# Four common PSUM banks, rewritten timetables, a bias moved and the layer norm's steps put in one order, in a two-layer vision kernel

## The chip, the cores and the metric

The kernel runs on one core of one Trainium2 chip. The metric is the device time of one execution in microseconds, the median of repeated runs. A core has TensorE (PE in the profile; its weight loads are PEld), VectorE (DVE), ScalarE (ACT), GpSimd (POOL) and SyncE (SP), which here issues nearly all DMA transfers in one queue. Each engine takes its instructions in program order and waits for others by semaphores. PSUM, where PE writes its products, has eight banks of 512 fp32 columns; SBUF is the larger on-chip memory.

## What is computed

The input is x of 8 images, 256 channels and 48 x 48 points (2304 tokens), all fp32. Two layers, each `x = x + layer(group_norm(x))`, with 32 groups of 8 channels:

- Layer 0 projects each token to features and to a position (256 each, with bias). Positions are normalised, the similarity of all pairs of tokens in an image is formed (2304 x 2304), each token takes its 16 most similar tokens, and the softmax of these 16 similarities weighs their features.
- Layer 1 is twice: a layer norm over channels, then a Mamba block without residual: in-projection to 512 + 512, a causal convolution over four tokens, SiLU, projections to a step size dt, B and C (16 states), the scan `h = exp(dt A) h + dt B x`, `y = C h` over the tokens, the skip `D x`, the gate `silu(z)`, and an out-projection to 256.

```
x = x + L0(gn(x))          # top-16 attention by similarity
x = x + L1(gn(x))          # twice: layer norm, Mamba block
```

## The kernel before

Layer 0 of the first image runs alone at the start. After that layer 1 of image b and layer 0 of image b + 1 run side by side, in an order written out by hand (`manual_schedule`): the program's order is each engine's order.

Layer 1 of an image is cut into 12 *units*: 6 chunks of 384 tokens (T) by 2 depths, in a skewed order. A unit has 16 *steps*, each 32 of the 512 inner channels with their 16 states laid over 128 partitions (4 states a row, Q), and a step has two *parts* of two states. So a unit has 32 parts, called places here, 96 units have 3072, and the main loop at the end of the kernel walks over them with m. At each place:

- `decay(m + 1)`: ACT writes exp(dt A) into one of two PSUM areas (L877).
- every second place `make_bx`: POOL multiplies B by dt x for the step after next (L853), and `pool_part` multiplies the states of the step before by C (L920).
- `run_scan(m)`: DVE runs the scan (L892). The letter of the part in the string SHARE says who multiplies by C: with G the scan is left in SBUF and POOL's L920 does it for one or both parts of the step; with V the scan is written to PSUM and DVE multiplies at once (L894). There are three strings, by what runs beside the unit: units 1 to 9 of an image except the last image have the top-k of the next image beside them (the first string); the units 0, 10 and 11 of these images have its projections (the second); the last image has nothing (the third).
- the other operations of a unit stand in timetables, lists of (place, operation): `between` goes ahead of the scan of a place and `behind` after it; `between_spare` and `behind_spare` take their part wherever no top-k stands beside. Places count from the unit's own first scan; -35 is a place in the unit before the previous one.
- `ahead.go(m)` moves layer 0 of the next image on by one step. A block of 128 tokens takes 16 places; the list `within` says at which of them each operation stands.

Operations that the change and the prediction touch:

- `load_rep` (L625) loads the dt or dt x rows of one step in four DMAs (tiles dtr, dtxr; three of each), `load_bc` (L633) B or C in four, `load_d` (L738) the skip weights, `times_x` makes dt x on POOL (L801) and stores it and dt (L804), `split` stores B and C (L776).
- `softplus` (L787 to L796) loads ACT's table, makes the four step sizes of a unit (L790) and puts the matmuls of the last two (L781) in between; `silu_z` (L815 to L819) does the like for the gate.
- the layer norm: `affine` (ACT, the group norm of the input, L670), `mean` (PE, L679), `center` (DVE, L685), `square` (ACT, L692), `variance` (PE, L698), `root` and `root_end`, `spread_root` (PE, L225), `scale` (DVE, L715), `normal` (ACT, L728). In the spare tables of before, square stands ahead of center and normal ahead of scale.
- `finish` (L540, L544): DVE adds the attended features, their bias and x in two operations of 128 columns, and takes the statistics of the sum; `leave` (L973) adds the last residual.
- PSUM: `mm` and `mm0` hand out banks of one ring; a new tile takes a bank that the program has given back. In the main loop da has four banks, the ring three, and `po`, which gathers the weighted features of a block over some six places, one of its own. While layer 0 runs alone, the ring has five and po two.

Of the kernel before, what the change touches and what calls it, by code (L numbers as in the profile page):

```python
# [8 lines left out]
F32 = mybir.dt.float32  # L9
BF16 = mybir.dt.bfloat16  # L10
AF = mybir.ActivationFunctionType
ALU = mybir.AluOpType
# [3 lines left out]
P = 128  # L16
# [9 lines left out]
def tile_conv_preact(  # L26
# [18 lines left out]
    nc = tc.nc  # L45
    B, C, N = x.shape
# [173 lines left out]

# [36 lines left out]

    def layer0(b, left, pool, ps0, alone):
        def mm0(w, name):
            return ps0.tile([P, 512], F32, tag="mm", name=name, bufs=5 if alone else 3)[:, :w]  # L260

        more = 2 if alone else 1
        depth = 2 if alone else 1
# [271 lines left out]
        def finish(t):  # L535
            row = blocks[t]
            xr = row["xr"]

            for cb in range(CB):
                nc.vector.scalar_tensor_tensor(  # L540
                    xr[:, cb, :], row["pr"][:, cb * P : (cb + 1) * P], b_feat[:, cb : cb + 1],
                    xr[:, cb, :], ALU.add, ALU.add,
                )
# [417 lines left out]
    def leave(unit, cb):  # L961

        b, c, rows = unit["b"], unit["c"], slice(cb * P, (cb + 1) * P)
        if unit["d"] + 1 < DEPTH:
            v1 = unit["left"].setdefault("v1", {})
            if c not in v1:
                v1[c] = hbm.tile([C, T], F32, tag="v1", name=f"v1_{b}_{c}", bufs=2 * BEHIND)
            vo = keep.tile([P, T], F32, tag="dtx", name=f"vo_{unit['u']}_{cb}")
            nc.scalar.copy(vo, unit["pw"][cb])
            nc.sync.dma_start(v1[c][rows, :], vo)  # L970
        else:
            res = unit["res"]
            nc.vector.tensor_add(res[:, cb, :], res[:, cb, :], unit["pw"][cb])  # L973
            nc.sync.dma_start(out[b, rows, c * T : (c + 1) * T], res[:, cb, :])


# [7 lines left out]
        (10, load_rep, "dtx", 9), (21, load_rep, "dtx", 14), (11, gate, 0), (-29, spread_root),  # L984
        (0, times_x, 3), (-19, load_in, 5), (33, load_out), (8, load_rep, "dtx", 8), (-22, load_in, 0),
        (21, load_rep, "dt", 13), (-20, tap, 0), (-10, step_size, 1), (9, copy_z, 2), (-18, in_proj, 2),
        (2, load_rep, "dtx", 5), (10, sum_states, 0), (13, load_rep, "dt", 9), (29, gate, 2), (9, silu_z),
        (7, load_rep, "dt", 6), (19, load_rep, "dt", 12), (-6, load_rep, "dtx", 1), (-14, load_in, 7),
        (-30, root), (9, load_rep, "dt", 7), (4, load_d, 1), (-24, load_in, 3), (17, load_rep, "dt", 11),
        (14, load_rep, "dtx", 11), (-13, x_proj), (-17, load_in, 6), (-3, load_d, 0), (4, load_rep, "dtx", 6),  # L990
        (-4, load_rep, "dtx", 2), (-42, load_v),
    ]
    behind = [
        (-12, split), (-3, load_rep, "dt", 1), (3, in_proj, 4), (-10, step_size, 0), (-3, load_rep, "dt", 0),
        (-8, load_rep, "dtx", 0), (-15, tap, 3), (-1, load_rep, "dt", 2), (-28, scale),
        (16, load_rep, "dtx", 12), (11, load_rep, "dt", 8), (8, in_proj, 6), (17, sum_states, 1),
        (-14, silu_x), (25, load_rep, "dt", 15), (-37, affine), (1, times_x, 2), (7, copy_z, 0),
        (10, load_rep, "dtx", 10), (-17, tap, 2), (-10, softplus), (-16, in_proj, 3), (3, load_rep, "dt", 4),
        (-29, load_in, 2), (6, in_proj, 7), (35, gate, 3), (-2, load_rep, "dtx", 3), (8, copy_z, 1),
        (40, leave, 1), (22, load_rep, "dtx", 15), (-8, load_in, 4), (29, load_d, 3), (-37, mean),  # L1000
        (-19, taps, 0), (-19, in_proj, 1), (-10, load_bc, 0), (33, sum_states, 3), (-30, root_end),
        (-9, times_x, 0), (-20, load_in, 1),
    ]
    between_spare = [
        (-34, center), (24, sum_states, 2), (-34, variance), (-21, in_proj, 0), (38, out_proj, 0),
        (-15, taps, 2), (-14, taps, 3), (-35, square), (39, leave, 0), (20, load_rep, "dt", 14),
        (5, load_rep, "dt", 5), (-4, load_bc, 1), (38, out_proj, 1), (17, load_d, 2), (-17, tap, 1),
        (18, load_rep, "dtx", 13), (-8, times_x, 1), (19, gate, 1), (-22, normal), (9, load_rep, "dtx", 8),
        (1, load_rep, "dt", 3), (0, load_rep, "dtx", 4), (14, load_rep, "dt", 10), (6, load_rep, "dtx", 7),
        (10, load_rep, "dtx", 9), (-18, taps, 0), (12, load_rep, "dtx", 10), (20, load_rep, "dtx", 14),  # L1010
        (11, gate, 0), (-1, times_x, 2), (-22, spread_root), (-19, load_in, 5), (33, load_out),
        (-22, load_in, 0), (21, load_rep, "dt", 13), (-20, tap, 0), (-10, step_size, 1), (9, copy_z, 2),
        (-18, in_proj, 2), (2, load_rep, "dtx", 5), (10, sum_states, 0), (13, load_rep, "dt", 9),
        (29, gate, 2), (9, silu_z), (7, load_rep, "dt", 6), (19, load_rep, "dt", 12), (-6, load_rep, "dtx", 1),
        (-14, load_in, 7), (37, gate, 3), (-31, root), (9, load_rep, "dt", 7), (5, load_d, 1),
        (-24, load_in, 3), (17, load_rep, "dt", 11), (14, load_rep, "dtx", 11), (-13, x_proj),
        (-17, load_in, 6), (-3, load_d, 0), (4, load_rep, "dtx", 6), (-4, load_rep, "dtx", 2), (-42, load_v),
    ]
    behind_spare = [
        (-12, split), (-3, load_rep, "dt", 1), (4, in_proj, 4), (-10, step_size, 0), (-5, load_rep, "dt", 0),  # L1020
        (-8, times_x, 3), (-8, load_rep, "dtx", 0), (-15, tap, 3), (-1, load_rep, "dt", 2), (-21, scale),
        (16, load_rep, "dtx", 12), (11, load_rep, "dt", 8), (8, in_proj, 6), (17, sum_states, 1),
        (-14, silu_x), (25, load_rep, "dt", 15), (-39, affine), (6, copy_z, 0), (-17, tap, 2), (-10, softplus),
        (-16, in_proj, 3), (7, in_proj, 5), (3, load_rep, "dt", 4), (-27, load_in, 2), (6, in_proj, 7),
        (-15, taps, 1), (-2, load_rep, "dtx", 3), (8, copy_z, 1), (40, leave, 1), (22, load_rep, "dtx", 15),
        (-16, load_in, 4), (29, load_d, 3), (-38, mean), (-21, in_proj, 1), (-12, load_bc, 0),
        (33, sum_states, 3), (-31, root_end), (-9, times_x, 0), (-25, load_in, 1),
    ]
    place = {(f, *args): part for part, f, *args in between + behind}

# [102 lines left out]
```

## Time and profile before

| | us |
|---|---|
| median of 3 runs | 9807.86 (9806.04 to 9808.63) |
| the profiled execution's own time | 9813.77 |
| its span | 9812.0 |
| first scan of the main loop starts at | 461.1 |
| DVE busy in the span | 8904.6 |
| POOL busy | 9023.9 |
| PE busy | 7958.7 |
| ACT busy | 7304.4 |

The profile is of one execution. Its page gives busy time by engine, the chain of work that ended last, and groups of equal instructions; a row of a group has the line, the engine, the operation, what it writes and reads, the shapes, the count, the busy time in us and the mean ns of one, and the idle time of the engine before it with what ended that. A row of the view of waits has engine and line that waited, what it waited for, the total in us, how often, and the longest. A row of the timeline has start and duration in us. Records of successive instructions of an engine overlap by some tens of ns, so the cost of one more instruction is read from the distance of starts.

### The profile page before, as it was taken

What the parts mean: (1) busy time and instruction counts of PE and PEld (TensorE: products, weight loads), DVE (VectorE), ACT (ScalarE), POOL (GpSimd) and SP (SyncE); (2) the same over time, 40 slices, a digit from 0 to 9 for tenths busy, and PEclk for the clock granted to TensorE, in tenths of its full rate; (3) what the DMA queues carried; (4) which work ended last, traced back from release to release, by engine and by line L of the source; (5) the groups of instructions that cost most, each with busy time, mean ns of one, the idle gap of its engine ahead of it and who ended that gap; (6) DMA issues with size and microseconds to landing.
All of it is one profiled execution on the core that took longest, in us unless ns stands there. A gap on an engine that the chain in (4) does not pass through costs nothing.

```text
span 9812.0 us, 133959 instructions
## 1 busy us (share of the span) xinstructions
PE 7958.7 (81%) x36761; PEld 4336.7 (44%) x36761; DVE 8904.6 (91%) x7864; ACT 7304.4 (74%) x15938; POOL 9023.9 (92%) x3971
## 2 busy tenths in 40 slices
PE   8888887888878887788877888778887788866665
PEld 6644443444434444444434445344443444422222
DVE  5599998999989999899988999899998999989898
ACT  4577877777777777777777787777786778767776
POOL 1199998999989999899999999999998999999999
PEclk9989998999989998899988999889998999977777
DMA  1244455545454445444454445544545454545554
GB/s 35 58 124 132 126 139 139 135 123 140 127 147 126 134 131 144 132 129 132 132 144 131 132 129 135 141 134 124 137 130 150 121 137 125 140 134 138 144 142 122
DMA packets 1241872, 1269.02 MB, mean 129 GB/s; under 512 B 266496, under 2 KB 1214208, under 8 KB 1241120
## 3 DMA queue, kind: packets, MB, share of 16 engines
q1 hardware_dynamic: 1240576, 1260.46, 47.7%
q8 instruction: 293, 4.80, 0.2%
q14 instruction: 459, 3.76, 0.1%
q10 hardware_dynamic: 544, 0.00, 0.0%
HBM read 1046.58 MB, written 212.86 MB: 128 GB/s over the span
## 4 chain that ended last, share of the span: by engine, by line
DVE 33%; ACT 24%; DMA 11%; PE 11%; SPq 10%; issue 7%; POOL 4%; ACTq 0%; DVEq 0%; POOLq 0%
DVE bx L892 11%; ACT da L877 10%; SPq L625 8%; DVE da L892 8%; DVE xc L751 5%; DMA dtr<-dt_d 4%; DVE bx L894 3%; DMA BC<-bc_d 3%; DVE top L464 2%; DVE left L467 2%; POOL bx L920 2%; PE po L514 2%; POOL bx L853 2%; DMA dtxr<-dtx_d 2%; ACT rest L486 1%
## 5 line engine op out<-in xcount | busy, mean ns | idle before, releaser
L853 POOL TENSOR_TENSOR bx<-BC,dtxr 128x1536 f32<-128x1536 f32 x1536 | 5296.3, 3454 | 144.5 <-PE y L938 72.8
L877 ACT ACTIVATE da<-dtr,A_sb 128x385 f32<-128x385 f32 x6144 | 3588.1, 584 | 868.6 <-DVE bx L892 375.1
L892 DVE TENSOR_TENSOR_SCAN bx<-da,bx 128x770 f32<-128x770 f32 x2073 | 3578.1, 1747 | 263.6 <-ACT da L877 232.4
L920 POOL TENSOR_TENSOR bx<-bx,BC 128x1536 f32<-128x1536 f32 (+1 forms) x1311 | 3353.6, 2558 | 70.5 <-DVE bx L892 66.0
L892 DVE TENSOR_TENSOR_SCAN da<-da,bx 128x770 f32<-128x770 f32 x999 | 1752.0, 1754 | 123.7 <-ACT da L877 81.2
L651 PE MATMUL pe<-vn,inw 128*128 128x384 f32 (+1 forms) x3072 | 1214.7, 526 | 329.6 <-issue 50.9
L514 PE MATMUL po<-feat,aT 128*128 128x256 f32 x5184 | 1352.3, 410 | 12.8 <-ACT aT L503 5.7
L938 PE MATMUL y<-bx,sel 128*32 128x384 f32 x12288 | 1266.0, 536 | 109.9 <-POOL bx L920 103.1
L443 PE MATMUL psim<-pos 128*128 128x512 f32 x2520 | 1215.2, 612 | 154.3 <-DVE xr L540 70.1
L514 PEld LDWEIGHTS po<-feat,aT 128*128 128x128 f32 x5184 | 1022.4, 203 | 343.1 <-issue 107.2
L894 DVE TENSOR_TENSOR bx<-da,BC 128x768 f32<-128x768 f32 x999 | 957.2, 958 | 34.4
L651 PEld LDWEIGHTS pe<-vn,inw 128*128 128x128 f32 x3072 | 566.9, 199 | 845.8 <-issue 206.2
L938 PEld LDWEIGHTS y<-bx,sel 128*32 128x32 f32 x12288 | 395.5, 118 | 961.5 <-issue 692.7
L443 PEld LDWEIGHTS psim<-pos 128*128 128x128 f32 x2520 | 478.0, 205 | 724.2 <-issue 375.5
L751 DVE SCALAR_TENSOR_TENSOR xc<-pe,cw,xc 128x384 f32<-128x384 f32 x1152 | 696.4, 611 | 43.4 <-ACT xc L743 16.3
L781 PE MATMUL pd<-dbl,dtp_sb 16*128 16x384 f32 x768 | 441.4, 689 | 336.5 <-ACT dt L790 189.9
L503 ACT ACTIVATE aT<-pt 128x512 f32<-128x512 f32 (+1 forms) x720 | 387.5, 548 | 419.8 <-PE pt L495 417.8
L956 PE MATMUL pw<-z,ow 128*128 128x384 f32 x1536 | 557.0, 509 | 112.8 <-ACT aT L503 52.4
L494 PE MATMUL pt<-ident,sim 128*128 128x128 f32 x2592 | 541.2, 290 | 18.5 <-ACT aT L503 13.6
L935 PE MATMUL y<-xc,dmat 128*128 128x384 f32 x768 | 398.3, 606 | 171.7 <-ACT h_st L930 58.5
L908 ACT COPY h_st<-da 128x2 f32<-128x2 f32 x808 | 128.6, 159 | 542.2 <-DVE bx L894 537.8
L495 PE MATMUL pt<-minus,rest 128*128 128x128 bf16 x2592 | 492.9, 224 | 5.9 <-ACT rest L486 5.8
(155 smaller groups left out, 9966.9 us busy)
## 6 DMA issues: line engine op xcount, KB each, us to landing
dtxr<-dtx_d SPq DMA_DIRECT2D x6144, 48.0 KB, 1.9
dtr<-dt_d SPq DMA_DIRECT2D x6144, 48.0 KB, 1.9
BC<-bc_d SPq DMA_DIRECT2D x768, 192.0 KB, 3.9
inw<-in_in_wT_dram SPq DMA_DIRECT2D x768, 128.0 KB, 2.3
dtx_d<-dtx SPq DMA_DIRECT2D x384, 192.0 KB, 2.3
dt_d<-dt SPq DMA_DIRECT2D x384, 192.0 KB, 2.3
ow<-in_out_wT_dram SPq DMA_DIRECT2D x96, 512.0 KB, 4.0
dmat<-diag SPq DMA_DIRECT2D x384, 64.0 KB, 2.2
```

Source lines behind the costliest of these rows:

```text
L443: nc.tensor.matmul(pm, pos[:, k, t * P : (t + 1) * P], pos[:, k, c0 : c0 + w], start=(k == 0), stop=(k == CB - 1),)
L514: nc.tensor.matmul(row["po"], aT[:, m % PT, :], feat[:, m, :], start=(m == 0), stop=(m == NB - 1))
L625: nc.sync.dma_start(rows[j * G : (j + 1) * G], src[:, i0, :])
L651: nc.tensor.matmul(pe, w[:, k], unit["vn"][:, k, lo:], start=(k == 0), stop=(k == CB - 1))
L751: nc.vector.scalar_tensor_tensor(unit["xc"][e], unit["pe"][e][:, k : k + T], cw[:, unit["d"], e, k : k + 1], unit["xc"][e], ALU.mult, ALU.add,
L853: nc.gpsimd.tensor_tensor(bx[:, :, 1:], unit["BC"][0], unit["dtxr"][i].unsqueeze(1).to_broadcast([P, Q, T]), ALU.mult,)
L877: nc.scalar.activation(da[:, s * (1 + T) : (s + 1) * (1 + T)], unit["dtr"][i], AF.Exp, scale=A_sb[:, unit["d"], i, p * HQ + s : p * HQ + s ...
L892: nc.vector.tensor_tensor_scan(h, da, g, 0.0, ALU.mult, ALU.add)
L894: nc.vector.tensor_tensor(bx[:, :, 0:T], da.rearrange("p (q t) -> p q t", q=HQ)[:, :, 1:], unit["BC"][1][:, qs], ALU.mult,)
L920: nc.gpsimd.tensor_tensor(g[:, :, 0:T], g[:, :, 1:], unit["BC"][1][:, qs], ALU.mult)
L938: nc.tensor.matmul(y[j * G : (j + 1) * G, :], sel, unit["bx"][k * J + j][:, q, 0:T], start=False, stop=True, skip_group_check=True,)
L956: nc.tensor.matmul(pw, unit["ow"][:, k, cb * P : (cb + 1) * P], unit["z"][k], start=(k == 0), stop=(k == DB - 1),)
```

## The change

- SHARE: in the first string place 29 goes from G to V, in the second 1 and 23 go from G to V, and 26 from V to G; in the third 11, 15 and 25 go from G to V, and 14, 18 and 27 from V to G.
- PSUM: the ring has four banks in the main loop and seven while layer 0 runs alone, and po takes its tile from it.
- The bias of the features is no longer added in `finish`; one sum of 256 columns takes the place of the two operations. The mean of the group norm gets it instead (`more` in `group_stats`), its shift is (bias - mean) x rstd, and `leave` adds it with the last residual.
- Timetables: `load_rep` of dt x 14 goes from place 21 to 19 (in the spare tables from 20 to 17), of dt 15 from 25 to 28, `affine` from -37 to -39, `times_x` of 2 from 1 to 2. In the spare tables center goes from -34 to -36, spread_root from -22 to -26 and scale from -21 to -25, so that center stands ahead of square, and scale ahead of normal.

```diff
     SHARE = (
-        "GGVGGGVVGGGGGGVGGGVVGGGVGGGGGGVG",
-        "GGGGVGVVGVVVGVGVGGGGVGVGGVVVGVGV",
-        "VGVGVGVGVGVGGGVGGGVVVGVVGGVVGGVG",
+        "GGVGGGVVGGGGGGVGGGVVGGGVGGGGGVVG",
+        "GVGGVGVVGVVVGVGVGGGGVGVVGVGVGVGV",
+        "VGVGVGVGVGVVGGGVGGGVVGVVGVVGGGVG",
     )
...
-    def group_stats(st, found, mm0, name):
+    def group_stats(st, found, mm0, name, more=None):
...
+        if more is not None:
+            nc.vector.tensor_add(mv[:, :, 0], mv[:, :, 0], more)
...
-        nc.gpsimd.tensor_mul(shift, mean, rstd)
-        nc.gpsimd.tensor_scalar(shift, shift, -1.0, None, ALU.mult)
+        if more is None:
+            nc.gpsimd.tensor_scalar(shift, mean, -1.0, None, ALU.mult)
+        else:
+            nc.gpsimd.tensor_sub(shift, more, mean)
+        nc.gpsimd.tensor_mul(shift, shift, rstd)
...
-            return ps0.tile([P, 512], F32, tag="mm", name=name, bufs=5 if alone else 3)[:, :w]
+            return ps0.tile([P, 512], F32, tag="mm", name=name, bufs=7 if alone else 4)[:, :w]
...
-                row["po"] = ps0.tile([P, 512], F32, tag="po", name=f"po_{b}_{t}", bufs=more)[:, :C]
+                row["po"] = mm0(C, f"po_{b}_{t}")
...
+            nc.vector.tensor_add(xr, xr, row["pr"].rearrange("p (k t) -> p k t", k=CB))
             for cb in range(CB):
-                nc.vector.scalar_tensor_tensor(
-                    xr[:, cb, :], row["pr"][:, cb * P : (cb + 1) * P], b_feat[:, cb : cb + 1],
-                    xr[:, cb, :], ALU.add, ALU.add,
-                )
                 nc.vector.bn_stats(st1[:, cb, t, :], xr[:, cb, :])
...
-        yield from group_stats(st1, found, mm0, f"b{b}")
+        yield from group_stats(st1, found, mm0, f"b{b}", b_feat)
...
-        return ps.tile([P, 512], F32, tag="mm", name=name, bufs=3)[:, :w]
+        return ps.tile([P, 512], F32, tag="mm", name=name, bufs=4)[:, :w]
...
-            nc.vector.tensor_add(res[:, cb, :], res[:, cb, :], unit["pw"][cb])
+            nc.vector.scalar_tensor_tensor(
+                res[:, cb, :], unit["pw"][cb], b_feat[:, cb : cb + 1], res[:, cb, :], ALU.add, ALU.add
+            )
...
     between = [
-        (21, load_rep, "dtx", 14)
...
     behind = [
-        (25, load_rep, "dt", 15), (-37, affine), (1, times_x, 2)
+        (28, load_rep, "dt", 15), (-39, affine), (2, times_x, 2), (19, load_rep, "dtx", 14)
...
     between_spare = [
-        (-34, center), (20, load_rep, "dtx", 14), (-22, spread_root)
+        (17, load_rep, "dtx", 14), (-36, center), (-26, spread_root)
...
     behind_spare = [
-        (-21, scale)
+        (-25, scale)
```

More of the change, by code (lines that the diff above doesn't have):

```diff
@@ L983, in tile_conv_preact @@
         (1, load_rep, "dt", 3), (0, load_rep, "dtx", 4), (15, load_rep, "dt", 10), (6, load_rep, "dtx", 7),
[L984 to L991, printed above, removed]
+        (10, load_rep, "dtx", 9), (11, gate, 0), (-29, spread_root), (0, times_x, 3), (-19, load_in, 5),
+        (33, load_out), (8, load_rep, "dtx", 8), (-22, load_in, 0), (21, load_rep, "dt", 13), (-20, tap, 0),
+        (-10, step_size, 1), (9, copy_z, 2), (-18, in_proj, 2), (2, load_rep, "dtx", 5), (10, sum_states, 0),
+        (13, load_rep, "dt", 9), (29, gate, 2), (9, silu_z), (7, load_rep, "dt", 6), (19, load_rep, "dt", 12),
+        (-6, load_rep, "dtx", 1), (-14, load_in, 7), (-30, root), (9, load_rep, "dt", 7), (4, load_d, 1),
+        (-24, load_in, 3), (17, load_rep, "dt", 11), (14, load_rep, "dtx", 11), (-13, x_proj),
+        (-17, load_in, 6), (-3, load_d, 0), (4, load_rep, "dtx", 6), (-4, load_rep, "dtx", 2), (-42, load_v),
     ]
@@ L996, in tile_conv_preact @@
         (16, load_rep, "dtx", 12), (11, load_rep, "dt", 8), (8, in_proj, 6), (17, sum_states, 1),
[L997 to L1000, printed above, removed]
@@ L1001, in tile_conv_preact @@
-        (-19, taps, 0), (-19, in_proj, 1), (-10, load_bc, 0), (33, sum_states, 3), (-30, root_end),
-        (-9, times_x, 0), (-20, load_in, 1),
+        (-14, silu_x), (28, load_rep, "dt", 15), (-39, affine), (2, times_x, 2), (7, copy_z, 0),
+        (19, load_rep, "dtx", 14), (10, load_rep, "dtx", 10), (-17, tap, 2), (-10, softplus),
+        (-16, in_proj, 3), (3, load_rep, "dt", 4), (-29, load_in, 2), (6, in_proj, 7), (35, gate, 3),
+        (-2, load_rep, "dtx", 3), (8, copy_z, 1), (40, leave, 1), (22, load_rep, "dtx", 15), (-8, load_in, 4),
@@ L1003, in tile_conv_preact @@
+        (29, load_d, 3), (-37, mean), (-19, taps, 0), (-19, in_proj, 1), (-10, load_bc, 0),
+        (33, sum_states, 3), (-30, root_end), (-9, times_x, 0), (-20, load_in, 1),
     ]
     between_spare = [
-        (-34, center), (24, sum_states, 2), (-34, variance), (-21, in_proj, 0), (38, out_proj, 0),
-        (-15, taps, 2), (-14, taps, 3), (-35, square), (39, leave, 0), (20, load_rep, "dt", 14),
-        (5, load_rep, "dt", 5), (-4, load_bc, 1), (38, out_proj, 1), (17, load_d, 2), (-17, tap, 1),
@@ L1008, in tile_conv_preact @@
[L1008 to L1016, printed above, removed]
+        (24, sum_states, 2), (-34, variance), (-21, in_proj, 0), (38, out_proj, 0), (-15, taps, 2),
@@ new lines, in tile_conv_preact @@
+        (-14, taps, 3), (-35, square), (39, leave, 0), (20, load_rep, "dt", 14), (5, load_rep, "dt", 5),
+        (-4, load_bc, 1), (38, out_proj, 1), (17, load_d, 2), (-17, tap, 1), (18, load_rep, "dtx", 13),
+        (-8, times_x, 1), (19, gate, 1), (-22, normal), (9, load_rep, "dtx", 8), (1, load_rep, "dt", 3),
+        (0, load_rep, "dtx", 4), (14, load_rep, "dt", 10), (6, load_rep, "dtx", 7), (10, load_rep, "dtx", 9),
+        (-18, taps, 0), (12, load_rep, "dtx", 10), (17, load_rep, "dtx", 14), (11, gate, 0), (-1, times_x, 2),
@@ new lines, in tile_conv_preact @@
+        (-19, load_in, 5), (33, load_out), (-22, load_in, 0), (21, load_rep, "dt", 13), (-20, tap, 0),
+        (-10, step_size, 1), (9, copy_z, 2), (-18, in_proj, 2), (2, load_rep, "dtx", 5), (10, sum_states, 0),
+        (13, load_rep, "dt", 9), (29, gate, 2), (9, silu_z), (7, load_rep, "dt", 6), (19, load_rep, "dt", 12),
+        (-6, load_rep, "dtx", 1), (-14, load_in, 7), (37, gate, 3), (-31, root), (9, load_rep, "dt", 7),
+        (5, load_d, 1), (-24, load_in, 3), (17, load_rep, "dt", 11), (14, load_rep, "dtx", 11), (-13, x_proj),
@@ L1017, in tile_conv_preact @@
         (-17, load_in, 6), (-3, load_d, 0), (4, load_rep, "dtx", 6), (-4, load_rep, "dtx", 2), (-42, load_v),
+        (-36, center), (-26, spread_root),
     ]
@@ L1020, in tile_conv_preact @@
         (-12, split), (-3, load_rep, "dt", 1), (4, in_proj, 4), (-10, step_size, 0), (-5, load_rep, "dt", 0),
-        (-8, times_x, 3), (-8, load_rep, "dtx", 0), (-15, tap, 3), (-1, load_rep, "dt", 2), (-21, scale),
+        (-8, times_x, 3), (-8, load_rep, "dtx", 0), (-15, tap, 3), (-1, load_rep, "dt", 2),
         (16, load_rep, "dtx", 12), (11, load_rep, "dt", 8), (8, in_proj, 6), (17, sum_states, 1),
@@ L1026, in tile_conv_preact @@
         (-16, load_in, 4), (29, load_d, 3), (-38, mean), (-21, in_proj, 1), (-12, load_bc, 0),
-        (33, sum_states, 3), (-31, root_end), (-9, times_x, 0), (-25, load_in, 1),
+        (33, sum_states, 3), (-31, root_end), (-9, times_x, 0), (-25, load_in, 1), (-25, scale),
     ]
```

## The prediction

> **What bounds the kernel now.** I read the page's busy shares and the chain first. Two engines, DVE and POOL, are busy over nine tenths of the span, and the chain still gives only a third to DVE and little to POOL: neither is a plain bound.
>
> ```profile
> PE 7958.7 (81%) x36761; PEld 4336.7 (44%) x36761; DVE 8904.6 (91%) x7864; ACT 7304.4 (74%) x15938; POOL 9023.9 (92%) x3971
> ...
> DVE 33%; ACT 24%; DMA 11%; PE 11%; SPq 10%; issue 7%; POOL 4%; ACTq 0%; DVEq 0%; POOLq 0%
> ```
>
> A share over the span mixes stages, so the next view is busy time in three stretches, placed by counting scans (32 to a unit; a place is a scan's number in its unit): nine units of the second image with the top-k of the next image beside them (I call this stage 0, 63 units in all), three units where that neighbour does its projections (stage 1, 21 units), and the last image (stage 2, 12 units).
>
> ```profile
> core 0: us, PE busy (x) PEld busy (x) DVE busy (x) ACT busy (x) POOL busy (x), PEclk, DMA share, GB/s
> 1754.60:2634.20 879.60, 758.01 (x3592) 418.58 (x3590) 847.08 (x739) 690.00 (x1514) 864.71 (x323) 0.94 0.49 131
> 2634.20:2940.50 306.30, 224.98 (x982) 117.34 (x986) 254.72 (x233) 217.45 (x470) 270.80 (x168) 0.84 0.52 141
> 8742.00:9780.00 1038.00, 644.34 (x2586) 271.02 (x2588) 940.20 (x798) 728.89 (x1602) 1015.53 (x424) 0.77 0.52 140
> ```
>
> Per unit, stage 0 lasts about 97.9 us with DVE idle 3.6 and POOL idle 1.7; stage 1 102.1 with DVE idle 17.2 and POOL idle 11.8; stage 2 86.9 with DVE idle 8.2 and POOL 1.9. In stage 0 POOL is the fuller engine, yet it runs ahead: its product of a step (L853) ended on average 4.5 to 19 us before the scan that reads it. POOL reaches DVE only indirectly. What ends the waits is in these rows:
>
> ```profile
> ACT da L877 <- DMA dtr<-dt_d: 255.3, 143, 4.3
> PE pd L781 <- ACT dt L790: 189.9, 96, 3.6
> ACT dt L790 <- PE pd L781: 82.8, 103, 1.3
> DVE v L685 <- ACT lsq L692: 30.7, 7, 10.1
> ```
>
> ```profile
> SPq L804 <- POOL dtx L801: 278.0, 163, 5.1
> ```
>
> The store of dtx waits for POOL and holds SP's queue; the step loads (dtr) behind it come late; ACT's decay waits for them; DVE's scan for the decay. That is POOL's way to the end.
>
> **The change, part by part.**
>
> *Shares.* By stage the V's (products with C done on DVE) go from 8, 15, 15 to 9, 16, 15 of 32. That is 63 + 21 = 84 more on DVE. Its price is read as a distance of starts:
>
> ```profile
> 3345.72 1.75 DVE L892 TENSOR_TENSOR_SCAN da<-da,bx 128x770 f32<-128x770 f32 x1
> 3347.51 0.96 DVE L894 TENSOR_TENSOR bx<-da,BC 128x768 f32<-128x768 f32 x1
> 3348.38 0.08 DVE L467 MATCH_VALUE_LOAD left<-top,sim 128x8 f32 x1
> 3348.45 2.54 DVE L467 MATCH_REPLACE8 left<-top,sim 128x2304 f32<-128x2304 f32 x1
> 3350.91 3.40 DVE L892 TENSOR_TENSOR_SCAN bx<-da,bx 128x770 f32<-128x770 f32 x2
> 3354.23 2.53 DVE L469 MAX8 top<-left 128x8 f32<-128x2304 f32 x1
> ```
>
> A V place takes 2.66 us to the next start (3348.38 - 3345.72), a G place 1.66 (half of 3.32, from 3350.91 to 3354.23): +0.98 us, the middle of 1.00 and the 0.96 of L894. On POOL a step with two G's becomes one with one:
>
> ```profile
> L920 POOL TENSOR_TENSOR bx<-bx,BC 128x1536 f32<-128x1536 f32 x762 | 2427.1, 3185 | 60.4 <-DVE bx L892 56.0 <-DVE den L479 1.0 <-DMA dtxr<-dtx_d 0.3
> L920 POOL TENSOR_TENSOR bx<-bx,BC 128x768 f32<-128x768 f32 x549 | 926.5, 1688 | 10.1 <-DVE bx L892 10.1
> L540 DVE SCALAR_TENSOR_TENSOR xr<-pr,b_feat,xr 128x128 f32<-128x128 f32 x288 | 96.0, 339 | 29.5 <-PE pr L531 29.3
> L973 DVE TENSOR_TENSOR xr<-xr,pw 128x384 f32<-128x384 f32 x96 | 51.5, 537 | 17.7 <-PE pw L956 16.0 <-DMA dtxr<-dtx_d 1.6
> ```
>
> 3.185 - 1.688 = 1.50 us, 84 x 1.50 = 126 us off POOL. In stage 2 four double and nine single steps become three and eleven: +0.19 us on POOL a unit.
>
> *Bias.* In finish two L540 operations of 128 columns become one sum of 256. A finish of before (two L540, two L544) takes 1.17 us from start to next scan. For the new sum I interpolate between L973 (384 columns, 0.45 us of starts where such an operation stands beside a G place) and L685 (768 columns, 0.88): 0.31. With two L544 at 0.245 (1.17 less two L540 at 0.34, halved) finish takes 0.80: 0.37 saved a block, two blocks a stage-0 unit, 0.74.[...] I take 0.37, since operations overlap here and starts are what counts[...]. In leave, L973 becomes the operation with a bias: nearest is L751 at the same width, 0.61 between starts against 0.45: +0.16, two to every second unit, +0.16 a unit. The extra add in the group norm is eight small operations, nothing.
>
> DVE's work so: stage 0 +0.98 - 0.74 + 0.16 = **+0.40 us a unit**, stage 1 +1.14, stage 2 +0.16. If no wait shrank, the change would cost 63 x 0.40 + 21 x 1.14 + 12 x 0.16 = 51 us.
>
> *Banks.* Before, three PSUM banks turn for everything and a fourth is for po alone; after, all four turn. By the bank numbers of the two built programs, pd 3 of a unit took the bank of the same unit's pd 0 or 1 in all 96 units, and does so in 7 units after, so its matmul no longer waits for the first softplus: ACT's 82.8 us (0.86 a unit) go. In stage 0 top-k on DVE covers them (DVE has no wait at places 21 to 28); in stages 1 and 2 DVE stands still there, at place 24, on average 3.6 and 2.8 us:
>
> ```profile
> 2813.72 1.76 DVE L892 TENSOR_TENSOR_SCAN bx<-da,bx 128x770 f32<-128x770 f32 x1 [6.64 <-ACT da L877]
> ```
>
> 0.86 x 21 = 18 us and 0.86 x 12 = 10 us saved. While po is held, three banks remain, as before, so I see no loss.
>
> *Timetables.* The stage-1 string gains V's at 1 and 23 and loses one at 26. Place 23 lies just ahead of that wait for softplus, so its 0.98 is hidden: 21 x 0.98 = 21 us back. Layer norm in order: center at -36 ahead of square at -35, scale at -25 ahead of normal at -22. Center no longer waits for ACT's square: the 30.7 us of the row above go. It waits for PE's mean at -38 instead, which in the units I looked at ended some 5 us ahead of that place. dtx 14 (four issues, 1.85 us of SP) moves from place 21 to 19, ahead of the store of bc_d, into time in which SP waits (place 18 to 21, some 7 us in unit 29). dt 15 moves from 25 to 28, behind dtx 1, the four BC loads and dtx 2, so its last issue goes out where dtx 2's does now. In nine stage-0 units that was on average 1.2 us ahead of the decay that reads dt 15 (place 30); a load lands 1.9 us after its issue, so it would come 0.7 late. The decay feeds a scan that the V at 29 sets back by 0.98: covered, so 0, with 1 us a unit as the bad end and 0.7 if that cover is gone. Behind dt 15 on SP stand an xr load and the next unit's dmat and dt 0; they keep their times. affine (two places earlier, ACT) gives PE's mean more room; PE waited 57.6 us for it with no one on DVE's path behind: 0. times_x 2 one place later: within POOL's own order, 0.
>
> *What POOL's relief returns in stage 0.* POOL is late at places 30 to 6, where times_x 2 and 3 and their stores stand; the new V at 29 takes 1.50 us off it just there. DVE waits at places 31 to 6 are about 1.9 us a unit; the rest (0.8 at place 13, behind ACT's silu of z) has nothing to do with POOL. No row shows how much returns: between 0 and 1.9. I take the middle, **1.0**.
>
> **Sum**, against the profiled span of 9812.0 (its own time 9813.8, 6 above the median; the difference is carried to the median): stage 0 63 x (0.40 - 1.0) = -38; stage 1 +24 - 21 - 18 - 31 = -46; stage 2 +2 + 2 - 10 = -6; first image, 18 shorter finishes where PE is 95% busy, -5. In all -95: 9808 - 95 = **9713 us**.
>
> **Rivals.** *POOL sets stages 0 and 1.* For it: 98% busy in stage 0, and SP's 278 us behind it. Against it: its product is done 4.5 us or more ahead. Then the 84 x 1.50 = 126 us return whole, with softplus (28) and half of the 31: -170, **9640**.
>
> *dt 15 comes late (slower).* The BC load that is now ahead of it on SP may start only when POOL has read the old BC; before, dt 15 did not stand behind that wait. Each microsecond by which it is later than its cover costs ACT's decay, and so the scan at place 30, 63 us in all. It decides from 95/63 = 1.5 us a unit; the four BC issues (1.85) with a landing slowed by 192 KB of BC (3.9 us against 1.9) make 2.0 the likely price: 9713 + 126 = **9839**. Against it: the margin above, and dtx 14 out of the same crowd.
>
> *The waits of stages 1 and 2 only move.* ACT's order is kept, so a wait of DVE that is taken away may come back at the next silu or load; then their savings (21 + 18 + 31 + 10) go and the work of 24 + 2 + 2 stays: -38 - 5 + 28 = -15, **9793**. For it: DVE's idle time there is spread over a dozen places. Against: place 24 alone holds a fifth of it.
>
> **How the numbers follow.** Chances: forecast 0.50 (own range 9670 to 9780, the lower end with all 1.9 us returned in stage 0, the upper with none), POOL 0.26, dt 15 late 0.13, waits that move 0.11. What a measurement tells from no change is about 0.2%, 20 us. Faster: 0.50 + 0.26 + 0.02 = 0.78; same 0.08 and slower 0.14 from the last two. The range runs from 9600 (POOL's case, with the waits for PE's y shrunk by 40) to 9825, which leaves out most of the dt 15 case.
>
> **What would show it.** Right: L894 x1083 and L892 into da x1083; POOL's busy time down by some 125;[...] no ACT dt <- PE pd row of 80 us; no DVE v <- ACT lsq row; SP's wait for POOL dtx well under 278. Right as a whole if stage 0 falls to about 97.3 us a unit and stage 1 to 99. Wrong: DVE's idle time in stage 0 still 3.5 us a unit, or ACT's wait for dtr grown past 255, above all at places 29 and 30; PE waiting for po's bank; DVE waiting for lm.

## The result, and the profile after

The kernel after takes 9697.99 us (median of 4 runs, 9694.31 to 9702.25) against 9806.95 (4 runs), a ratio of 0.9889 with a 95% interval of 0.9872 to 0.9907: 109 us less. The forecast was 9713. Its profiled execution has a span of 9700.2 us against 9812.0. The code of the units stands two lines lower in it: L877 of before is L879 now, L892 is L894, L894 is L896, L973 is L975. Layer 0 stands five lower (L336 is L341), and L540 has become L544.

The page of the kernel after, busy time by engine and the chain that ended last:

```profile
PE 7965.7 (82%) x36761; PEld 4443.6 (46%) x36761; DVE 8964.8 (92%) x7812; ACT 7309.1 (75%) x16018; POOL 8901.3 (92%) x3983
...
DVE 42%; ACT 18%; PE 12%; issue 9%; DMA 9%; SPq 7%; POOL 3%; ACTq 0%; DVEq 0%; POOLq 0%
```

POOL has lost 122.6 us and DVE has gained 60.2, near what the counts said (126 and 51). DVE's share of the chain is up from 33% to 42%, and what stood for DMA, SP and ACT is down. The same three stretches as before (stage 0 of the second image, its stage 1, the last image), and the groups whose cost the prediction had to guess:

```profile
core 0: us, PE busy (x) PEld busy (x) DVE busy (x) ACT busy (x) POOL busy (x), PEclk, DMA share, GB/s
1730.00:2607.40 877.40, 772.88 (x3610) 434.82 (x3608) 853.46 (x733) 693.08 (x1527) 855.82 (x326) 0.92 0.49 132
2607.40:2899.70 292.30, 218.74 (x985) 118.87 (x986) 258.57 (x239) 216.55 (x469) 262.48 (x165) 0.82 0.53 146
8650.30:9686.90 1036.60, 651.54 (x2608) 276.17 (x2611) 945.58 (x800) 734.24 (x1615) 1019.44 (x435) 0.77 0.51 139
```

```profile
L896 DVE TENSOR_TENSOR bx<-da,BC 128x768 f32<-128x768 f32 x1083 | 1037.8, 958 | 37.3
...
L544 DVE TENSOR_TENSOR xr<-xr,pr 128x256 f32<-128x256 f32 x144 | 59.3, 412 | 31.8 <-PE pr L536 31.5
L975 DVE SCALAR_TENSOR_TENSOR xr<-pw,b_feat,xr 128x384 f32<-128x384 f32 x96 | 57.7, 601 | 5.8 <-PE pw L958 5.8
L194 DVE TENSOR_TENSOR mv_b<-mv_b,b_feat 128x2 f32<-128x2 f32 x8 | 16.2, 2029 | 0.3
```

In stage 1 (the second stretch) DVE now stands still 33.7 us in three units, where it stood 51.6: most of the gain is there. In stage 0 it is 23.9 in nine units, after 32.5. (The stretches of before lie 5 to 14 us beside their units' scans; by the scans DVE's idle time there is the same to 0.1 us.) The last row is a surprise: an addition of two columns takes 2 us, and its 16.2 us were in no count. The rows that ended waits, and SP's own:

```profile
ACT da L879 <- DMA dtr<-dt_d: 149.8, 108, 5.3
...
PE pd L783 <- ACT dt L792: 17.6, 7, 3.1
...
DVE v L687 <- PE lm L681: 13.3, 2, 8.0
...
ACT dt L792 <- PE pd L783: 4.7, 6, 0.8
...
PE po L519 <- ACT dt L792: 34.6, 42, 2.0
```

```profile
SPq L806 <- POOL dtx L803: 373.9, 232, 3.5
```

ACT's wait for pd has gone from 82.8 to 4.7 us and PE's for the step sizes from 189.9 to 17.6, as predicted. ACT's wait for dtr fell from 255.3 to 149.8, but SP's wait for POOL's dtx, which was to fall from 278.0, rose to 373.9. Two signs of being wrong that the prediction had named are there as well. At place 30 of stage 0, where ACT never waited for a load in before, it now waits 1.5 us a unit. And PE waits for a bank for po, 34.6 us in all, behind the softplus (the last row; before has no such row): a part of PE's wait has moved from the step sizes to po. DVE's wait for lm, a third such sign, stood at 7.9 us in before already.

### The profile page after: what moved, and what is told of

It reads as the page before. It is cut to its first block, busy times and chain, and to the rows that moved or that the text cites. A ratio compares the mean times of both kernels' runs of the same rounds, so it can differ in the third digit from the quotient of the medians.

```text
span 9700.2 us, 133631 instructions
## 1 busy us (share of the span) xinstructions
PE 7965.7 (82%) x36761; PEld 4443.6 (46%) x36761; DVE 8964.8 (92%) x7812; ACT 7309.1 (75%) x16018; POOL 8901.3 (92%) x3983
## 4 chain that ended last, share of the span: by engine, by line
DVE 42%; ACT 18%; PE 12%; issue 9%; DMA 9%; SPq 7%; POOL 3%; ACTq 0%; DVEq 0%; POOLq 0%
DVE bx L894 14%; DVE da L894 10%; ACT da L879 7%; DVE xc L753 6%; SPq L627 5%; DVE top L469 3%; DVE bx L896 3%; DMA BC<-bc_d 3%; PE psim L448 3%; DVE left L472 2%; DMA dtxr<-dtx_d 2%; PE y L940 2%; POOL bx L855 2%; DMA dtr<-dt_d 2%; ACT rest L491 2%
## 5 line engine op out<-in xcount | busy, mean ns | idle before, releaser
L855 POOL TENSOR_TENSOR bx<-BC,dtxr 128x1536 f32<-128x1536 f32 x1536 | 5299.4, 3456 | 129.5 <-PE y L940 89.6
L879 ACT ACTIVATE da<-dtr,A_sb 128x385 f32<-128x385 f32 x6144 | 3596.2, 586 | 1076.9 <-DVE bx L894 670.0
L894 DVE TENSOR_TENSOR_SCAN bx<-da,bx 128x770 f32<-128x770 f32 x1989 | 3432.8, 1748 | 160.7 <-ACT da L879 138.6
L922 POOL TENSOR_TENSOR bx<-bx,BC 128x1536 f32<-128x1536 f32 (+1 forms) x1323 | 3231.3, 2442 | 112.2 <-DVE bx L894 102.0
L894 DVE TENSOR_TENSOR_SCAN da<-da,bx 128x770 f32<-128x770 f32 x1083 | 1900.7, 1755 | 91.5 <-ACT da L879 61.9
L940 PE MATMUL y<-bx,sel 128*32 128x384 f32 x12288 | 1293.5, 538 | 142.0 <-POOL bx L922 123.5
L519 PE MATMUL po<-feat,aT 128*128 128x256 f32 x5184 | 1355.7, 410 | 48.8 <-ACT dt L792 34.6
L896 DVE TENSOR_TENSOR bx<-da,BC 128x768 f32<-128x768 f32 x1083 | 1037.8, 958 | 37.3
L448 PEld LDWEIGHTS psim<-pos 128*128 128x128 f32 x2520 | 504.6, 212 | 662.6 <-issue 404.6
L700 PE MATMUL lv<-ones_mean,lsq 128*128 128x1 f32 x1152 | 220.8, 319 | 465.1 <-ACT lsq L694 428.5
L958 PE MATMUL pw<-z,ow 128*128 128x384 f32 x1536 | 540.7, 499 | 44.7 <-DVE z L946 23.9
L499 PEld LDWEIGHTS pt<-ident,sim 128*128 128x128 f32 x2592 | 381.6, 147 | 289.1 <-ACT sim L457 70.8
```

What stands on the lines that cost most here:

```text
L448: nc.tensor.matmul(pm, pos[:, k, t * P : (t + 1) * P], pos[:, k, c0 : c0 + w], start=(k == 0), stop=(k == CB - 1),)
L499: nc.tensor.transpose(pt[:, q], row["sim"][:, r], ident)
L519: nc.tensor.matmul(row["po"], aT[:, m % PT, :], feat[:, m, :], start=(m == 0), stop=(m == NB - 1))
L855: nc.gpsimd.tensor_tensor(bx[:, :, 1:], unit["BC"][0], unit["dtxr"][i].unsqueeze(1).to_broadcast([P, Q, T]), ALU.mult,)
L879: nc.scalar.activation(da[:, s * (1 + T) : (s + 1) * (1 + T)], unit["dtr"][i], AF.Exp, scale=A_sb[:, unit["d"], i, p * HQ + s : p * HQ + s ...
L894: nc.vector.tensor_tensor_scan(h, da, g, 0.0, ALU.mult, ALU.add)
```

## The experiments

The table has all kernels. A unit is measured from its first scan to that of the next, in the profiled execution, and averaged over the 63 units of stage 0, the 21 of stage 1 and the 12 of stage 2 (the last unit to the end of its last scan). A wait of DVE is put down to the place whose scan stands ahead of it, so the prediction's wait for softplus at place 24 is that of place 23 here. Ratios are to runs of before in the same session, with the 95% interval.

| kernel | median us | ratio | stage 0 | stage 1 | stage 2 |
|---|---|---|---|---|---|
| before | 9806.95 | | 97.97 | 101.08 | 86.88 |
| after | 9697.99 | 0.9889 [0.9872, 0.9907] | 97.72 | 96.69 | 86.38 |
| banks alone | 9728.02 | 0.9924 [0.9907, 0.9940] | 97.99 | 96.96 | 86.86 |
| shares alone | 9766.97 | 0.9966 [0.9955, 0.9977] | 97.97 | 99.41 | 86.55 |
| bias alone | 9804.89 | 0.9999 [0.9992, 1.0006] | 97.77 | 101.50 | 86.91 |
| timetables alone | 9853.65 | 1.0053 [1.0038, 1.0068] | 98.34 | 101.29 | 87.66 |
| after less banks | 9803.30 | 0.9998 [0.9989, 1.0007] | 98.08 | 100.04 | 86.85 |
| after less shares | 9756.66 | 0.9953 [0.9938, 0.9968] | 97.93 | 97.88 | 87.23 |
| after less bias | 9703.46 | 0.9899 [0.9884, 0.9913] | 97.98 | 96.06 | 86.57 |
| after less timetables | 9652.05 | 0.9847 [0.9832, 0.9861] | 97.23 | 95.69 | 86.45 |
| after, times_x 2 back | 9686.54 | 0.9880 [0.9865, 0.9895] | 97.65 | 96.85 | 86.18 |
| after, times_x 2 and dt 15 back | 9671.54 | 0.9866 [0.9850, 0.9883] | 97.33 | 96.43 | 86.13 |
| old timetables, layer norm in order | 9669.06 | 0.9859 [0.9843, 0.9876] | 97.33 | 96.43 | 86.27 |
| the same, bias added on GpSimd | 9668.94 | 0.9859 [0.9844, 0.9874] | 97.31 | 96.18 | 86.29 |

What is left out: in every kernel with the timetables of before, before itself among them, the layer norm of 33 units (those where it stands without top-k beside) takes the variance of values not yet centred, and normal reads them ahead of scale, so that the reciprocal deviation is not applied there. The instructions are the same in number and size; only their order and what waits for what differ. The kernels with the new timetables have the right order, and so have the last two rows.

**The banks alone.**

```diff
-            return ps0.tile([P, 512], F32, tag="mm", name=name, bufs=5 if alone else 3)[:, :w]
+            return ps0.tile([P, 512], F32, tag="mm", name=name, bufs=7 if alone else 4)[:, :w]
...
-                row["po"] = ps0.tile([P, 512], F32, tag="po", name=f"po_{b}_{t}", bufs=more)[:, :C]
+                row["po"] = mm0(C, f"po_{b}_{t}")
...
-        return ps.tile([P, 512], F32, tag="mm", name=name, bufs=3)[:, :w]
+        return ps.tile([P, 512], F32, tag="mm", name=name, bufs=4)[:, :w]
```

> Before with the four common banks alone. My sum: only softplus is shortened, 18 us in stage 1 and 10 in stage 2, nothing in stage 0 and in the first image: 9780, and ACT's wait for PE's pd (82.8 us) gone. Rival, banks are what moved stage 1 (it fell by 92 us in the changed kernel where I had 46): 40 to 80 us there, 9720 to 9760. Rival, four banks help only with tables made for them: within 20 us of before.

78 us less by the medians, and in the profiled execution 87 less in stage 1 (21 units by 4.12) and nothing elsewhere. The softplus, from one table load of ACT to the next, fell from 4.21 to 3.31 us in all stages (in unit 0 of the images but the last from 5.34 to 4.28), the 0.9 foreseen. Part of what exceeds it can be read in unit 11 of an image, where DVE's idle time falls from 20.6 to 12.3 us (mean of images 1 to 5, counted from 0): 6.64 to 5.36 at the wait for softplus, and 3.41 to 0.27 at place 29, where center stands. The timeline of before there; a row has start, duration, engine, operation, and in brackets the idle time before it and its releaser:

```profile
2826.51 2.93 PE L336 MATMUL pp<-xt,w 128*128 128x384 f32 x4 [3.23 <-DVE z L944]
...
2829.47 0.58 ACT L363 ACTIVATE pos<-pp,b_pos 128x384 f32<-128x384 f32 x1 [3.35 <-PE pp L336]
...
2831.96 0.83 ACT L692 ACTIVATE lsq<-v 128x768 f32<-128x768 f32 x1
...
2832.82 0.96 DVE L685 TENSOR_TENSOR v<-lm,v 128x768 f32<-128x768 f32 x1 [3.70 <-ACT lsq L692]
```

and that of the banks alone, at the same place of the same unit:

```profile
2797.45 2.74 PE L336 MATMUL pp<-xt,w 128*128 128x384 f32 x8
...
2802.08 0.56 ACT L363 ACTIVATE pos<-pp,b_pos 128x384 f32<-128x384 f32 x1
...
2804.54 0.83 ACT L692 ACTIVATE lsq<-v 128x768 f32<-128x768 f32 x1
...
2805.40 0.96 DVE L685 TENSOR_TENSOR v<-lm,v 128x768 f32<-128x768 f32 x1 [0.24 <-ACT lsq L692]
```

With three banks the second position projection had to wait until DVE's gate had read its bank; ACT's copy of it stood in ACT's queue ahead of the square, and center waited for the square. With four banks the two projections run together (x8). The row of DVE's wait for the square, 30.7 us in before, is now

```profile
DVE v L685 <- ACT lsq L692: 10.0, 7, 8.6
```

with no step of the layer norm moved: two thirds of it was a wait for a bank, at the end of a chain of three engines. Over stage 1 the waits of places 23 and 29 make 35 of the 87 us. The rest lies in all three units (in all 51 of the 87 in unit 11, 23 in unit 10, 12 in unit 0) and was not followed back to a bank. In stage 2 the wait did move: DVE's wait at place 23 fell from 2.80 to 1.97 us and that at place 10 rose from 2.35 to 3.20.

**The shares alone.** The three strings as in the diff of the change.

```diff
-        "GGVGGGVVGGGGGGVGGGVVGGGVGGGGGGVG",
-        "GGGGVGVVGVVVGVGVGGGGVGVGGVVVGVGV",
-        "VGVGVGVGVGVGGGVGGGVVVGVVGGVVGGVG",
+        "GGVGGGVVGGGGGGVGGGVVGGGVGGGGGVVG",
+        "GVGGVGVVGVVVGVGVGGGGVGVVGVGVGVGV",
+        "VGVGVGVGVGVVGGGVGGGVVGVVGVVGGGVG",
```

> Before with the new strings alone. My sum: stage 0 +0.98 - 1.0 a unit, nothing; stage 1 +0.98 - 0.98, nothing: 9800 to 9815, POOL's busy time 126 us less and DVE's 82 more. Rival, POOL sets the pace: 126 us less, 9680. Rival, DVE sets it: 60 to 82 us more, 9868 to 9890.

39 us less than before, 35 of it in stage 1 (0 was foreseen) and none in stage 0, as foreseen. In stage 0 DVE's work rose by 0.85 us a unit and POOL's fell by 1.30, and DVE's waits fell from 2.60 to 1.84. In before, ACT stood still for a load of dtr ahead of the decays of places 0 and 6, 3.0 us a unit in all, and the scans of these two places waited 1.04 us a unit for ACT. Here ACT waits 0.8 there, and the scans' wait is gone. The rows of the path, which in before have 255.3 and 278.0:

```profile
ACT da L877 <- DMA dtr<-dt_d: 93.1, 95, 5.3
```

```profile
SPq L804 <- POOL dtx L801: 174.1, 161, 3.5
```

This is the way from POOL to DVE that the prediction drew: POOL, the store of dtx in SP's queue, the load of dtr, the decay, the scan. Against it the gate's wait for PE's y at place 3 grew from 0.17 to 0.58. In stage 1 the V at 23 was indeed hidden: in unit 11 the wait behind it fell from 6.64 to 5.68. The V at 1 seems to be hidden too, which the prediction did not count: the wait at place 6 fell from 2.91 to 0.79. No run changes one letter alone.

**The bias alone.**

```diff
+            nc.vector.tensor_add(mv[:, :, 0], mv[:, :, 0], more)
...
+            nc.vector.tensor_add(xr, xr, row["pr"].rearrange("p (k t) -> p k t", k=CB))
             for cb in range(CB):
-                nc.vector.scalar_tensor_tensor(
-                    xr[:, cb, :], row["pr"][:, cb * P : (cb + 1) * P], b_feat[:, cb : cb + 1],
-                    xr[:, cb, :], ALU.add, ALU.add,
-                )
...
-            nc.vector.tensor_add(res[:, cb, :], res[:, cb, :], unit["pw"][cb])
+            nc.vector.scalar_tensor_tensor(
+                res[:, cb, :], unit["pw"][cb], b_feat[:, cb : cb + 1], res[:, cb, :], ALU.add, ALU.add
+            )
```

> Before with the bias moved alone. My sum: DVE 0.74 - 0.16 = 0.58 us less in each of 63 stage-0 units, 5 less in the first image, 0.16 more in 33 units: -37, 9770.[...] Rival, POOL sets stage 0: within 15 us of before.

No change: 0.9999. In stage 0 DVE's busy time fell by 0.48 us a unit (0.58 foreseen), but the unit only by 0.20: DVE's waits grew from 2.60 to 2.91. Stage 1 lost 9 us. The time is where the rival (POOL sets stage 0) put it, but the shares alone took 1.30 us a unit off POOL, put 0.85 on DVE, and left stage 0 as it was: it follows neither engine's work by itself.

**The timetables alone.** The entries that change, without their neighbours in the lists:

```diff
-        (25, load_rep, "dt", 15), (-37, affine), (1, times_x, 2), (21, load_rep, "dtx", 14)
+        (28, load_rep, "dt", 15), (-39, affine), (2, times_x, 2), (19, load_rep, "dtx", 14)
...
-        (-34, center), (20, load_rep, "dtx", 14), (-22, spread_root), (-21, scale)
+        (-36, center), (17, load_rep, "dtx", 14), (-26, spread_root), (-25, scale)
```

> Before with the four new timetables alone (places of loads, affine, times_x, and the layer norm in order where no top-k stands beside). My sum: the 30.7 us of DVE waiting for ACT's square go, all in stage 1: 9777. Rival, the tables carry most of stage 1's fall: 60 to 90 us, 9720 to 9750. Rival, dt 15 behind the BC load comes late without the V at 29 as cover: 0.7 us a stage-0 unit, +44.

Slower by 47 us, the wrong way: +23 in stage 0, +4 in stage 1, +9 in stage 2. This was the first sign that a term put at 0 was not 0. The rival with dt 15 is there, but smaller than it was priced: without the V at 29 as cover the scan of place 30, which never waited for its decay in before, waits 0.25 us a unit, not 0.7, so 16 us in stage 0. The gate's wait at place 3 grew too, from 0.17 to 0.71. That the sum comes near the rival's 44 is chance.

**The change without its timetables.**

> The changed kernel with the four timetables of before. The tables alone cost 47 us. If the parts add up: 9698 - 47 = 9651, faster than both. If the tables fit the new strings and banks (the parts alone sum to -71, together -109, so 38 us of interplay): undoing them costs up to 38 - 47 + 47, between 9690 and 9740. My sum had 31 us in them: 9729.

9652: the new timetables cost 46 us at the end, as they do alone (in the profiled executions 31 in stage 0 and 21 in stage 1). Stage 0, where banks, shares and bias alone gave 0, 0 and 0.20 us a unit, gains 0.74 with all three; stage 1 is the sum of the three to 0.02 us.

**The change without its banks, without its shares, without its bias.** In each the lines of that part are those of before.

> The changed kernel with three banks and one for po. Banks alone gave 78 us, all in stage 1. If the parts add up: 9776. If the new tables need the fourth bank (alone with three, PE's variance waited 154 + 87 us for a bank, against 49 before): worse than that, 9790 to 9830. My sum had 28: 9726.

> The changed kernel with the strings of before. Shares alone gave 39 us, 35 of them in stage 1. If the parts add up: 9737. If the new tables (dt 15 after the V at 29) need the strings: 9740 to 9790, with stage 0 above 98.2 us a unit. Rival, POOL is no longer late with four banks: 9698, same.

> The changed kernel with the bias added in finish again. Alone the move gave 1 us: stage 0 13 less, stage 1 9 more. If the parts add up: 9699, same. If DVE is nearer to setting stage 0 now that POOL has 1.5 us less: my 0.58 us a unit, 37 more, 9735.

Without the banks the other three parts give nothing (0.9998): the banks are worth 105 us at the end and 78 alone. The shares are worth 59 at the end and 39 alone, the bias 5, which its interval does not tell from nothing. In stage 0 banks and shares give nothing alone, but 22 and 13 us at the end: they help one another there, though no run has just these two. The wait at place 3 shows a part of it: with the new shares the gate waits for PE's y 0.58 us a unit, with banks and bias as well 0.36 (the change without its timetables); in the kernel after it is 0.66, and without the banks 0.99.

**times_x 2 back at place 1.**

```diff
-        (2, times_x, 2)
+        (1, times_x, 2)
```

> The kernel after with one entry of the timetable put back: times_x 2 at place 1 (an odd place) instead of 2 in the 63 units with top-k beside; dt 15 at 28, dtx 14 at 19 and 17, affine at -39 and the new layer norm order stay. Theory: the 46 us that the new timetables cost on top of the other three parts come from this entry, because at an even place GpSimd has make_bx and its part of the top-k queued ahead of times_x 2, so that the copies of dtx and with them ScalarE's da come late: 9652 to 9667 us, SyncE's wait for GpSimd's dtx falls from 373.9 us to about 170, ScalarE's wait for the copies from 149.8 to about 125, and the gain lies in the 63 units (97.7 to about 97.2 us each). Rival: dt 15 three places later, or the layer norm order of the 33 other units, carries the loss: 9690 to 9700 us, with SyncE's wait gone all the same.

9686.5 (9680.2 to 9701.3): 11 of the 46 us, and the 11 are not clear of the scatter (the profiled execution, which the table's stages come from, was the slowest of the four). The mechanism was there: in stage 0 POOL started times_x 2 at place 2.5 in before, 4.3 in after (it stood behind an L855 and an L922, the two products that POOL has at an even place) and 2.0 here; SP's wait for dtx fell from 373.9 to 293.5. It was not what set the time. The theory fell; the gate's wait at place 3 was still 0.70.

**dt 15 back at place 25 as well.**

```diff
-        (28, load_rep, "dt", 15)
+        (25, load_rep, "dt", 15)
```

> The kernel after with times_x 2 back at place 1 and, beyond that, dt 15 back at place 25; affine at -39, dtx 14 at 19 and 17 and the new layer norm order stay. Theory: with dt 15 at 28 ScalarE idles 1.47 us a unit ahead of the decay at place 30 (0.00 with it at 25), and although the scan at place 30 still finds its decay ready, what stands behind in ScalarE's queue is late, down to PE's y at place 3 of the next unit, for which VectorE's gate waits 0.70 us against 0.38: putting it back gives the 0.3 us a unit, 9663 to 9672 us, the time of the old tables with the layer norm in order (9669.06), with VectorE's wait at place 3 near 0.38 and ScalarE's idle time at place 30 near 0. Rival: affine two places earlier or dtx 14 at its new places carries the rest: 9680 to 9690 us, with the waits at places 3 and 30 gone all the same.

9671.5, as the theory said. ACT's timeline at place 30 of one unit of stage 0, first with dt 15 at 28:

```profile
2217.63 1.20 ACT L879 ACTIVATE da<-dtr,A_sb 128x385 f32<-128x385 f32 x2 [0.94 <-DMA dtr<-dt_d]
2218.77 0.18 ACT L932 COPY h_st<-bx 128x4 f32<-128x4 f32 x1
2218.85 1.33 ACT L491 ACTIVATE rest<-left,three 128x512 bf16<-128x512 f32 x2
```

and with it at 25:

```profile
2202.36 1.19 ACT L879 ACTIVATE da<-dtr,A_sb 128x385 f32<-128x385 f32 x2
2203.48 0.18 ACT L932 COPY h_st<-bx 128x4 f32<-128x4 f32 x1
2203.57 1.33 ACT L491 ACTIVATE rest<-left,three 128x512 bf16<-128x512 f32 x2
```

ACT stands still for the load ahead of this decay, 1.47 us a unit on average with dt 15 at 28, nothing with it at 25. The scan that reads the decay hardly waits for it (0.04 us a unit; the decay was ready 1.01 us ahead on average). What is late is behind it on ACT: the copies and the top-k's remainder, and then PE. The gate's wait for y at place 3 falls from 0.70 to 0.44 us a unit. That PE is late because of these ACT operations was argued from their order and not tested by itself. The two steps together, 26 us, are clear of the scatter; how they share it is not, and no run has dt 15 back without times_x 2. SP's wait for dtx is still 288.0 us here, where it is 165.9 in the change without its timetables and 168.3 in the next kernel, which takes as long: this wait had become idle time that costs nothing.

**The layer norm's order, and where the bias is added.** The change with the timetables of before, in which only center, spread_root and scale of the spare tables are put in order; then the same with the two-column addition on GpSimd.

```diff
-        (-34, center), (-22, spread_root), (-21, scale)
+        (-36, center), (-26, spread_root), (-25, scale)
```

```diff
-            nc.vector.tensor_add(mv[:, :, 0], mv[:, :, 0], more)
+            nc.gpsimd.tensor_add(mv[:, :, 0], mv[:, :, 0], more)
```

> The kernel after with the timetables of the kernel before, in which only the layer norm steps of the 33 units without top-k beside are put in the order of the kernel after (center at -36, spread_root at -26, scale at -25, all last in their lists); it computes the reference. Theory: the order costs nothing, as center moves only two places back and the two others wait for work that is long done: 9650 to 9660 us, as with the old tables (9652.05), stage 1 at 95.7 us a unit. Rival: the order is what costs stage 1 its 1.0 us a unit (96.69 against 95.69) and the last stage nothing: 9670 to 9680 us.

> As the run before it, and the two-column addition of the bias to the group norm's means (L194) on GpSimd instead of VectorE. Theory: the addition takes 2.3 us on VectorE in seven of its eight places (0.161 us in the first image, where GpSimd is idle)[...]; on GpSimd it runs between GpSimd's own operations and VectorE has no such operation to wait in: 5 to 16 us below the run before it, all in stage 1, most in the unit at place 0 or 11 of an image that holds the addition. Rival: VectorE would idle for those 2.3 us anyway, as stage 1 is set by waits for PE and ScalarE: within 5 us of the run before it, with VectorE's wait elsewhere longer by as much.

The order costs 17 us (9652.05 to 9669.06), nearest to its rival (in the profiled executions 15 in stage 1 and 6 in stage 0). With the right order the in-projection depends on scale as well as on normal, and the waits of the kernel with the order put right show it:

```profile
PE pe L653 <- ACT vn L730: 60.7, 20, 6.7
PE pe L653 <- DVE v L717: 9.2, 11, 1.6
```

Without it they are 44.2 us and no row. Which of the moved steps, or which wait, makes the 17 us was not tested. This is the price of computing what the reference asks. The kernel with the order right, 9669, is 29 us below the kernel after; the one that follows and the one before it (9671.5) are level with it. So 46 us are accounted for: 11 and 15 for times_x 2 and dt 15, in this order of undoing, and 17 for the layer norm, with 2 or 3 for affine and dtx 14, less than the runs can tell from nothing.

The addition takes 0.195 us on GpSimd in all eight places, and the time does not move: DVE's busy time in stage 1 falls by 0.79 us a unit and its idle time rises by 0.54. The rival held.

## Why the prediction was right, and which of its steps were not

The time was 15 us from the forecast, but that is in part luck: stage 0 fell 22 us too little and stage 1 46 us too much, and the two errors largely cancel. The prediction's own sign of being right as a whole, about 97.3 us a unit in stage 0 and 99 in stage 1, did not come: they are 97.72 and 96.69. By stage, against the sum of the prediction:

| | foreseen | measured | banks alone | shares alone | bias alone | timetables alone |
|---|---|---|---|---|---|---|
| stage 0 | -38 | -16 | +1 | 0 | -13 | +23 |
| stage 1 | -46 | -92 | -87 | -35 | +9 | +4 |
| stage 2 | -6 | -6 | 0 | -4 | 0 | +9 |
| first image | -5 | +2 | -1 | +2 | +3 | +4 |

- *Work on the engines: right.* L896 x1083, POOL -122.6 us. The finish sum took 412 ns on average. Between starts a finish of before took 1.17 us and takes 0.85: 0.32 saved, where 0.37 was taken. The operation with a bias in leave costs 0.06 us more between starts (0.454 to 0.516), not 0.16. But less work was not less time: alone, the bias returned 0.20 us of the 0.58 a unit foreseen for stage 0.
- *Stage 0, what POOL's relief returns (1.0 us): right for the shares,* whose added work came back, by the path that was drawn. Without the new timetables the stage gains 0.74 against the 0.60 foreseen, though with the help of the banks, which were put at 0 there. The step that failed is "times_x 2 ... 0" and "dt 15 ... covered, so 0": the two cost 26 us together by the medians, and 25 in stage 0 alone by the profiled executions. I had the load late by 0.7 us and bounded it at the scan that reads it. ACT waits 1.5 us a unit for it in the kernel after, and the scan behind the V at 29 only 0.05: the cover did what was said, and the loss seems to come by way of ACT's queue. The rival "dt 15 comes late" had the place and ACT's wait, but not the path, and its price of 2.0 us a unit was 0.24 (15 us by 63).
- *Stage 1, banks (18 us) and layer norm order (31 us): the sum was mis-sized, 49 against 87 for the banks alone,* and the 31 had the wrong cause for two thirds. The row of waits named the last engine of a chain; the bank at its start was what to undo. What the other 52 of the 87 are was not followed. The layer norm's order does not save, it costs 17.
- *Stage 1, shares: mis-sized.* The V at 23 was hidden as said; the V at 1 was counted as plain work and seems to be hidden too. The stage fell by 35 us where 0 was foreseen.
- *Stage 2: right in sum (-6), wrong in its terms.* The 10 us of the banks moved to place 10, as the rival of moving waits said for this stage; it fell for stage 1.
- *The rival in which POOL sets the time* fell in the shares alone: POOL's busy time fell by 120 us and the kernel's by 39, none of it in stage 0. In the kernel after SP's wait for dtx even rose, and the kernel was faster.
- *"The extra add in the group norm is ... nothing"* was right in time and wrong in duration: 2.18 to 2.37 us in seven of its eight places (below).
- *First image -5:* +2. Its shorter finishes gave nothing.

## What to carry to other kernels

When a row of waits looks like an order of operations, follow the releaser back one engine at a time: here a wait of DVE for ACT was a wait of ACT for PE, and that one of PE for a bank. When a load is moved to a later place, ask not only whether its reader on the fullest engine still has cover, but also what stands in the queue of the engine that stops for it. An edit of several parts that comes out as forecast should still be taken apart: here one part gave back 46 of the 153 us that the others saved.

## What the hardware showed beside that

The addition of the bias to the group norm's mean has two inputs of two columns in SBUF. In the first image, while GpSimd stood idle, it took 0.161 us. In the seven others it took 2.18 to 2.37 us, and each ended within 0.02 us of the end of a GpSimd product. The timeline of after, one of the seven and the first:

```profile
1486.16 2.30 DVE L194 TENSOR_TENSOR mv_b<-mv_b,b_feat 128x2 f32<-128x2 f32 x1
...
1485.02 3.42 POOL L855 TENSOR_TENSOR bx<-BC,dtxr 128x1536 f32<-128x1536 f32 x1 [1.08 <-DMA dtxr<-dtx_d]
...
400.91 0.16 DVE L194 TENSOR_TENSOR mv_b<-mv_b,b_feat 128x2 f32<-128x2 f32 x1
```

1486.16 + 2.30 and 1485.02 + 3.42 are 1488.46 and 1488.44: VectorE's addition ended with GpSimd's product. VectorE's other sums and products of two tensors in the main loop read one side from PSUM, and none ran so long over its usual time: L896 took 957 to 962 ns in all its 1083 places, L544 397 to 422 in all its 144. That GpSimd's product held the addition is inferred from the seven ends and from the 0.161 us of the first image. The cause was not shown; no run moved an operand of the addition to PSUM.
